# Regrouping float32r and float16 passes inside the gate products of a gated graph network on Trainium2

## The chip, the cores and the metric

The kernel runs on one core of one Trainium2 chip. The metric is the device time of one launch in microseconds (us); smaller is better. TensorE (PE in the profile) does the matrix products, ScalarE (ACT) and VectorE (DVE) the elementwise work, GpSimd (POOL) a little of it, and SyncE (SP) issues the transfers. PEld is the part of TensorE that loads a stationary operand (the weights of a matmul) into the array.

## What is computed

There are 64 graphs of 256 nodes with 256 features. A layer of three gated graph steps is followed by a graph attention layer; both begin with a layer norm and a ReLU and end with a residual. The gates of the gated steps are where the change lies:

```python
for i in range(3):
    m = einsum('bnd,de->bne', h, weight[i])
    aggr = einsum('bst,bsd->btd', A, m)          # A = (adj != 0)
    gi = aggr @ w_ih.T + b_ih ;  gh = h @ w_hh.T + b_hh
    r = sigmoid(i_r + h_r) ;  z = sigmoid(i_z + h_z)
    n = tanh(i_n + r * h_n)
    h = (1 - z) * n + z * h
...
e = leaky(h' @ a_left + (h' @ a_right).T), masked by adj
out = x + softmax(e) @ (h' @ W.T)
```

## The kernel before, in words

**Tiling.** The 64 graphs go in 32 pairs. For one pair, the state h is held transposed: two tiles (one for each block of 128 features, `db`) of 128 partitions by 512 columns, where the 512 columns are the 2 x 256 nodes of the two graphs. `weight[i] @ w_ih.T` is multiplied together once at the start, so that a gated step needs only the propagation by the adjacency matrix (`prop`, L807) and the gates. The stationary operand of a gate product is a 128 x 128 block of a weight matrix, and the moving operand is a 128 x 512 tile of the state. In the last gated step of the last pair the two graphs are done apart, so that the products there have 256 columns.

**Products in three parts.** A value v is split (`split16`, L655) into v0, which is rounded to float32r by ScalarE, a remainder v1 in float16 by VectorE (L660, L662), and a combination vd of both in float32r (L664). The weights are split likewise into `fac[m][:, 0]` (float32r), `low[m]` (float16) and `fac[m][:, 1]` (float32r). A gate (`gate`, L676) is then made of three operations on one PSUM bank:

- `top` (L683 to L686): for each term (the state's part `hh`, the aggregated part `i`, or both) and each of the two blocks `kb` of the contraction, a float32r matmul (j = 0) and a float16 matmul (j = 1), all accumulated in the bank. A top of one term has two of each kind; a top of two terms (gate z) has four of each.
- `scale` (L700): one ScalarE activation, in place, over the bank.
- `rest` (L688 to L691): two float32r matmuls for each term, accumulated on what `scale` left.

One `db` of one gated step has the gates r, nh, ni and z, where the top of r is made in two pieces (`topT`, `topF`): five tops, four scales and four rests. With 2 blocks, 3 steps and 32 pairs, and the last step of the last pair doubled, that is 970 tops, with 2,328 float32r and 2,328 float16 matmuls on L686, 582 scales in all and 2,328 float32r matmuls on L691. Gates r and z end in a Tanh on ScalarE (L826, L839); nh and ni go to VectorE (L831, L834), then to a Tanh (L836) and three VectorE operations (L843 to L847), which make the new state.

In the built program a float16 matmul stands as two instructions, a `Ldweights` and a `Matmult`; a float32r matmul is one instruction that loads its own weights. The profile shows a weight load (PEld) for both.

**What sets the order.** All operations are given to a planner (`Plan`) with an engine, an assumed duration, the buffers that they read and write, and a priority made of due times and a table of leads. `Plan.run` (L286) places them one by one, by the earliest start that its own durations give, and calls each operation's function at that moment; each engine executes its instructions in the order in which they were placed. So the order across gates is fixed when the program is built, and the tops, scales and rests of several gates, the propagation and the attention of other pairs lie interleaved on TensorE. The function `pe` (L431) registers a TensorE operation. The eight PSUM banks are one class of buffers of the planner (`bank`).

Of the kernel before, what the change touches and what calls it, by code (L numbers as in the profile page):

```python
# [353 lines left out]
def tile_gated_gnn_then_gat(  # L354
# [44 lines left out]
    DB = D // P  # L399
# [11 lines left out]
    plan = Plan(WINDOW, LEAD)  # L411
# [16 lines left out]

    def pe(name, n, fn, **kw):  # L431
        return plan.op(name, "PE", n, n + 220, fn, **kw)

    def act(name, n, fn, **kw):
        plan.op(name, "ACT", n, n + 170, fn, **kw)
# [54 lines left out]
    def setup():  # L490
# [6 lines left out]
        def load_rows():  # L497
# [4 lines left out]
        plan.op("rows", "ACT", 200, 3000, load_rows, w=[(rw, ONE)])  # L502
        pt = Buf("bank")
        pe("vec t", TR, lambda: nc.tensor.transpose(pt.t[:, :nrow], rw.t, ident[:nrow, :nrow]),
           r=[(rw, ONE), ("ident", ONE)], w=[(pt, ONE)])
        dve("vec", 70, lambda: nc.vector.tensor_copy(vec, pt.t[:, :nrow]), r=[(pt, ONE)], w=[("vec", ONE)])
# [14 lines left out]
        def transposed(dst, region, blocks, whole=None, up=1.0):  # L521

            def go_for(c):
                pt = Buf("bank")

                def go():
                    for r, (b, k) in enumerate(blocks):
                        nc.tensor.transpose(pt.t[:, ts(r, P)], parts(b)[:, k, ts(c, P)], ident)

                n = len(blocks)  # L530
                pe("w turn", TR * n, go, r=[(b, ONE) for b, _ in blocks] + [("ident", ONE)], w=[(pt, ONE)])
                w = n * P if whole is None else whole

                def copies():
                    nc.scalar.activation(dst(c)[:, :w], pt.t[:, :w], AF.Copy, scale=up)
                    if w < n * P:
                        nc.scalar.activation(dst(c)[:, w:], pt.t[:, w : n * P], AF.Copy, scale=0.5 * up)

                act("w copy", (140 if w == n * P else 260) + n * 110, copies, r=[(pt, ONE)], w=[region(c)])

            for c in range(DB):
                go_for(c)
# [46 lines left out]
        def bank_of(blocks, c):  # L589

            pt = Buf("bank")

            def go():
                for r, (b, k) in enumerate(blocks):
                    nc.tensor.transpose(pt.t[:, ts(r, P)], parts(b)[:, k, ts(c, P)], ident)

            pe("w turn", TR * len(blocks), go, r=[(b, ONE) for b, _ in blocks] + [("ident", ONE)], w=[(pt, ONE)])
            return pt
# [70 lines left out]
    def fit(ns, part):  # L669

        return ns if len(part) == 2 else 80 + 0.5 * ns

    def columns(part):
        return slice(part[0] * N, (part[-1] + 1) * N)

    def gate(name, e, terms, tops, apart=False, bias=0.0, part=ALL):  # L676

        bank = Buf("bank")
        half = e // 3
        cols, cost, cost16 = columns(part), PASS if len(part) == 2 else PROP, PASS16 if len(part) == 2 else PROP16  # L680
        f = lambda m, j, kb: low[m][:, kb, ts(e, P)] if j == 1 else fac[m][:, j // 2, kb, ts(e, P)]

        def top(terms, first):  # L683
            seq = [(m, j, kb, s[kb][j]) for m, s in terms for kb in range(DB) for j in range(2)]
            for n, (m, j, kb, b) in enumerate(seq):
                nc.tensor.matmul(bank.t[:, cols], f(m, j, kb), b.t[:, cols], start=(first and n == 0), stop=True, skip_group_check=True)  # L686

        def rest():  # L688
            for m, s in terms:
                for kb in range(DB):  # L690
                    nc.tensor.matmul(bank.t[:, cols], f(m, 2, kb), s[kb][2].t[:, cols], start=False, stop=True, skip_group_check=True)  # L691

        def reads(js, half_, terms=terms):
            return [(s[kb][j], ONE) for _, s in terms for kb in range(DB) for j in js] + [
                (f"fac{m}", tuple((kb, half, half_) for kb in range(DB))) for m, _ in terms]

        for ts_ in [terms[:1], terms[1:]] if apart and len(terms) > 1 else [terms]:
            tops.append(pe(name + " top" + (str(len(ts_) < len(terms) and ts_[0] is terms[0])[0]), 2 * (cost + cost16) * len(ts_), lambda ts_=ts_: top(ts_, ts_[0] is terms[0]),
                           r=reads((0, 1), 0, ts_), w=[(bank, ONE)]))
        act(name + " scale", fit(575 if "nh" in name else 515, part), lambda: nc.scalar.activation(  # L700
            bank.t[:, cols], bank.t[:, cols], AF.Identity, bias=bias, scale=SPLIT + 1.0), r=[("vec", ONE)], w=[(bank, ONE)])
        pe(name + " rest", 2 * cost * len(terms), rest, r=reads((2,), 1), w=[(bank, ONE)])
        return bank
# [361 lines left out]
```

## Time and profile before

The median of three runs is 2061.08 us (2057.64 to 2062.22). In the profiled execution the span is 2060.2 us, and the granted TensorE clock is 0.998 on average.

| What | Instructions | Busy us | Share of the span |
|---|---|---|---|
| TensorE, matmuls | 9,965 | 2039.5 | 99% |
| TensorE, weight loads | 9,965 | 1317.1 | 64% |
| ScalarE | 3,043 | 1744.2 | 85% |
| VectorE | 3,890 | 1699.6 | 82% |
| GpSimd | 198 | 147.8 | 7% |

A row of the profile's groups is read as: line, engine, operation, output<-inputs by the program's names without buffer numbers, shapes, count | busy us in all, mean ns of one | idle time of the engine just before, and what ended it. A row of the timeline has start (us from the beginning of the span), duration, and then the same names; neighbours of one kind are merged, with their number behind the x. float32r operands are shown as f32, with the tile name `round`. The recorded end of a matmul is modelled by the profiler, and matmuls are pipelined: the recorded duration of one is longer than the distance to the next. The pace of TensorE is therefore read from distances between neighbours, not from durations.

### The profile page before, as it was taken

What the parts mean: (1) busy time and instruction counts of PE and PEld (TensorE: products, weight loads), DVE (VectorE), ACT (ScalarE), POOL (GpSimd) and SP (SyncE); (2) the same over time, 40 slices, a digit from 0 to 9 for tenths busy, and PEclk for the clock granted to TensorE, in tenths of its full rate; (3) what the DMA queues carried; (4) which work ended last, traced back from release to release, by engine and by line L of the source; (5) the groups of instructions that cost most, each with busy time, mean ns of one, the idle gap of its engine ahead of it and who ended that gap; (6) DMA issues with size and microseconds to landing.
All of it is one profiled execution on the core that took longest, in us unless ns stands there. A gap on an engine that the chain in (4) does not pass through costs nothing. (4 is left out here: it accounts for less than half of the span.)

```text
span 2060.2 us, 31404 instructions
## 1 busy us (share of the span) xinstructions
PE 2039.5 (99%) x9965; PEld 1317.1 (64%) x9965; DVE 1699.6 (82%) x3890; ACT 1744.2 (85%) x3043; POOL 147.8 (7%) x198
## 2 busy tenths in 40 slices
PE   8999999999999999999999999999999999999998
PEld 5666666666666666666666656666666666666666
DVE  7678888888788888888888888888888888888886
ACT  6688888888888888888888888888888888888875
POOL 1000000000000000000000000000000000000000
PEclk9999999999999999999999999999999999999999
DMA  4137776677865677765677765678756778666632
GB/s 127 32 78 130 137 118 115 117 121 131 144 109 113 117 129 128 131 118 112 116 133 134 122 115 112 120 131 143 112 113 119 123 129 141 108 116 112 112 70 62
DMA packets 734472, 239.44 MB, mean 116 GB/s; under 512 B 658257, under 2 KB 734305, under 8 KB 734305
## 3 DMA queue, kind: packets, MB, share of 16 engines
q1 hardware_dynamic: 734272, 237.41, 65.3%
q8 instruction: 79, 1.29, 0.3%
q14 instruction: 89, 0.72, 0.1%
q10 hardware_dynamic: 32, 0.01, 0.0%
HBM read 61.09 MB, written 16.84 MB: 38 GB/s over the span
## 5 line engine op out<-in xcount | busy, mean ns | idle before, releaser
L686 PE MATMUL bank<-round,fac 128*128 128x512 f32 (+1 forms) x1164 | 551.1, 543 | 0.0
L686 PE MATMUL bank<-round,fac_hh 128*128 128x512 f32 (+1 forms) x1164 | 534.2, 522 | 0.0
L686 PE MATMUL bank<-half,low_hh 128*128 128x512 f16 (+1 forms) x1164 | 451.6, 388 | 0.0
L686 PE MATMUL bank<-half,low 128*128 128x512 f16 (+1 forms) x1164 | 450.5, 388 | 0.0
L691 PE MATMUL bank<-round,fac_hh 128*128 128x512 f32 (+1 forms) x1164 | 435.4, 455 | 0.6 <-ACT bank L700 0.4
L700 ACT ACTIVATE bank<-bank 128x512 f32<-128x512 f32 (+1 forms) x582 | 334.8, 580 | 116.3 <-PE bank L686 115.6
L691 PE MATMUL bank<-round,fac 128*128 128x512 f32 (+1 forms) x1164 | 367.3, 409 | 2.5 <-ACT bank L700 2.5
L724 ACT COPY full<-full 128x1024 uint16<-128x1024 uint16 x304 | 354.3, 1165 | 17.2 <-DMA full<-full 15.8
L686 PEld LDWEIGHTS <-low 128*128 128x128 f16 x1164 | 111.5, 96 | 293.8 <-issue 292.9
L686 PEld LDWEIGHTS <-low_hh 128*128 128x128 f16 x1164 | 111.8, 96 | 293.1 <-issue 291.6
L664 DVE SCALAR_TENSOR_TENSOR round<-half,round 128x512 fp32r<-128x512 f16 x384 | 260.4, 686 | 1.3
L691 PEld LDWEIGHTS bank<-round,fac 128*128 128x128 f32 x1164 | 216.5, 189 | 52.8 <-ACT bank L700 8.3
L686 PEld LDWEIGHTS bank<-round,fac_hh 128*128 128x128 f32 x1164 | 230.1, 198 | 14.6
L686 PEld LDWEIGHTS bank<-round,fac 128*128 128x128 f32 x1164 | 231.0, 198 | 8.7
L691 PEld LDWEIGHTS bank<-round,fac_hh 128*128 128x128 f32 x1164 | 211.5, 193 | 26.3 <-ACT bank L700 12.7
L746 POOL TENSOR_TENSOR small<-small,nhalf 128x2 f32<-128x2 f32 x128 | 114.4, 895 | 1526.3 <-DVE small L744 1456.0
L807 PE MATMUL bank<-round,round 128*128 128x256 f32 x1536 | 218.4, 291 | 0.3 <-DVE round L885 0.3
L831 DVE SCALAR_TENSOR_TENSOR full<-full,bank 128x512 f32<-128x512 f32 (+1 forms) x194 | 130.5, 673 | 106.9 <-ACT full L826 78.8
L845 DVE SCALAR_TENSOR_TENSOR full<-full,full 128x512 f32<-128x512 f32 (+1 forms) x194 | 132.3, 682 | 92.4 <-ACT full L839 92.0
L807 PEld LDWEIGHTS bank<-round,round 128*128 128x128 f32 x1536 | 201.2, 191 | 5.5 <-DVE round L885 0.5
L836 ACT ACTIVATE full<-full,vec 128x512 f32<-128x512 f32 (+1 forms) x194 | 136.3, 717 | 29.8 <-DVE full L834 29.7
L658 ACT ACTIVATE round<-bank 128x512 fp32r<-128x512 f32 x192 | 114.8, 598 | 49.6 <-PE bank L807 48.7
(108 smaller groups left out, 2958.8 us busy)
## 6 DMA issues: line engine op xcount, KB each, us to landing
full<-full SPq DMA_DIRECT2D x484, 128.0 KB, 3.5
x<-in_x_dram SPq DMA_DIRECT2D x64, 256.0 KB, 3.2
adj<-in_adj_dram SPq DMA_DIRECT2D x64, 256.0 KB, 5.2
full<-in_x_dram SPq DMA_DIRECT2D x64, 256.0 KB, 3.3
full<-full SPq DMA_DIRECT2D x248, 64.0 KB, 2.9
out_dram<-full SPq DMA_DIRECT2D x62, 256.0 KB, 2.5
full<-line SPq DMA_DIRECT2D x62, 128.0 KB, 3.8
full<-full SPq DMA_TRANSPOSE x304, 3.3
```

The source lines that it names most:

```text
L658: act(name + " 0", A512 if bank else C512, lambda: nc.scalar.activation(v0.t, v.t, AF.Copy, scale=up), r=[(v, ALL)], w=[(v0, ONE)])
L664: dve2(name + " d", V512, lambda: nc.vector.scalar_tensor_tensor(vd.t, v1.t, -SPLIT, v0.t.bitcast(F32), op0=ALU.mult, op1=ALU.add), r=[(v0 ...
L686: nc.tensor.matmul(bank.t[:, cols], f(m, j, kb), b.t[:, cols], start=(first and n == 0), stop=True, skip_group_check=True)
L691: nc.tensor.matmul(bank.t[:, cols], f(m, 2, kb), s[kb][2].t[:, cols], start=False, stop=True, skip_group_check=True)
L700: act(name + " scale", fit(575 if "nh" in name else 515, part), lambda: nc.scalar.activation(bank.t[:, cols], bank.t[:, cols], AF.Identity ...
L724: act(name, 1065, lambda: nc.scalar.copy(dst.t.bitcast(U16).rearrange("p (j n b) -> p j n b", j=2, b=2), src.t.bitcast(U16).rearrange(f"p ...
L746: pool(name + " pow", 900, lambda: nc.gpsimd.tensor_tensor(sm.t[:, 16:18], sm.t[:, 16:18], nhalf, ALU.pow), r=[("nhalf", ONE)], w=[(sm, (2 ...
L807: nc.tensor.matmul(pa.t[:, ts(g, N)], b, parts(A[g])[:, sb, :], start=(n == 0), stop=(n == len(terms) - 1))
L831: dve(f"u {db}{of}", fit(S512, part), lambda u=u, k=ph, b=r_, cols=cols: nc.vector.scalar_tensor_tensor(u.t[:, cols], b.t[:, cols], 1.0, k ...
L836: act(f"tanh {db}{of}", fit(615, part), lambda u=u, en=en, cols=cols: nc.scalar.activation(u.t[:, cols], u.t[:, cols], AF.Tanh, bias=b_i[: ...
L845: dve2(f"d mul {db}{of}", fit(V512, part), lambda d=d, b=z_, cols=cols: nc.vector.scalar_tensor_tensor(d.t[:, cols], b.t[:, cols], 1.0, d. ...
```

## The change

Before, the matmuls of a top alternate: for each term and each `kb`, a float32r matmul and then a float16 matmul. After, all matmuls of one kind in a top come first, then all of the other kind. A flag `narrow` remembers whether the last TensorE operation placed was a top that ended in float16; if so, the next top begins with its float16 matmuls, so that the two tops share one float16 group. Any TensorE operation that is not a top clears the flag. The purpose is to have TensorE change less often between the two kinds of operand. The assumed durations given to the planner are the same as before, and so are the number and the size of all instructions.

```diff
+    narrow = [False]
+
-    def pe(name, n, fn, **kw):
-        return plan.op(name, "PE", n, n + 220, fn, **kw)
+    def pe(name, n, fn, mixed=False, **kw):
+        def go():
+            fn()
+            narrow[0] = narrow[0] and mixed
+
+        return plan.op(name, "PE", n, n + 220, go, **kw)
...
         def top(terms, first):
-            seq = [(m, j, kb, s[kb][j]) for m, s in terms for kb in range(DB) for j in range(2)]
+            js = (1, 0) if narrow[0] else (0, 1)
+            narrow[0] = js[-1] == 1
+            seq = [(m, j, kb, s[kb][j]) for j in js for m, s in terms for kb in range(DB)]
             for n, (m, j, kb, b) in enumerate(seq):
                 nc.tensor.matmul(bank.t[:, cols], f(m, j, kb), b.t[:, cols], start=(first and n == 0), stop=True, skip_group_check=True)
...
-            tops.append(pe(name + " top" + ..., 2 * (cost + cost16) * len(ts_), lambda ts_=ts_: top(ts_, ts_[0] is terms[0]),
+            tops.append(pe(name + " top" + ..., 2 * (cost + cost16) * len(ts_), lambda ts_=ts_: top(ts_, ts_[0] is terms[0]), mixed=True,
                            r=reads((0, 1), 0, ts_), w=[(bank, ONE)]))
```

More of the change, by code (lines that the diff above doesn't have):

```diff
@@ L697, in gate @@
         for ts_ in [terms[:1], terms[1:]] if apart and len(terms) > 1 else [terms]:
-            tops.append(pe(name + " top" + (str(len(ts_) < len(terms) and ts_[0] is terms[0])[0]), 2 * (cost + cost16) * len(ts_), lambda ts_=ts_: top(ts_, ts_[0] is terms[0]),
+            tops.append(pe(name + " top" + (str(len(ts_) < len(terms) and ts_[0] is terms[0])[0]), 2 * (cost + cost16) * len(ts_), lambda ts_=ts_: top(ts_, ts_[0] is terms[0]), mixed=True,
                            r=reads((0, 1), 0, ts_), w=[(bank, ONE)]))
```

## The prediction

> **What bounds the kernel now.** I read the page's engine shares first, then who waits for whom, then the pace of TensorE in the timeline. The shares (engine, busy us, share, instructions):
>
> ```profile
> PE 2039.5 (99%) x9965; PEld 1317.1 (64%) x9965; DVE 1699.6 (82%) x3890; ACT 1744.2 (85%) x3043; POOL 147.8 (7%) x198
> ```
>
> 99% alone proves little, since pipelined matmuls overlap in the record. The waits decide (waiter <- releaser: us in all, times, longest):
>
> ```profile
> PEld L686 <- issue: 584.5, 2278, 0.4
> ...
> ACT bank L700 <- PE bank L686: 146.8, 262, 2.2
> ...
> PEld bank L691 <- ACT bank L700: 21.0, 86, 1.0
> ...
> PE bank L691 <- ACT bank L700: 2.9, 8, 0.5
> ```
>
> ScalarE waits 146.8 us for the tops; TensorE's matmul stream waits 2.9 us for the scales. The other engines follow TensorE. Differencing the recorded ends of all neighbouring matmuls gives the same: distances more than 20 ns over the median of their kind sum to 27 us, about 7.4 of them at 20 rests behind a scale, most others in the start and the last 50 us. So the time is a sum of matmul distances, and what counts is one distance. A steady stretch of TensorE:
>
> ```profile
> 1001.53 1.09 PE L691 MATMUL bank<-round,fac 128*128 128x512 f32 x4
> 1002.46 0.40 PE L686 MATMUL bank<-round,fac 128*128 128x512 f32 x1
> 1002.70 0.39 PE L686 MATMUL bank<-half,low 128*128 128x512 f16 x1
> 1002.74 0.58 PE L686 MATMUL bank<-round,fac 128*128 128x512 f32 x1
> 1003.17 0.39 PE L686 MATMUL bank<-half,low 128*128 128x512 f16 x1
> 1003.21 0.58 PE L686 MATMUL bank<-round,fac_hh 128*128 128x512 f32 x1
> ```
>
> Four float32r in a row take 1002.46 - 1001.53 = 0.93 us, 232.5 ns each. A float32r/float16 pair repeats after 1003.21 - 1002.74 = 0.47 (0.464 over five pairs), so a float16 matmul behind a float32r one also costs about 232. Over the whole trace, ends 2,280 times float32r to float16: mean 232.5, median 233 ns; float16 to float32r: 232.6, 233; float32r to float32r: median 234. Then the weight loads of the same stretch:
>
> ```profile
> 1002.70 0.10 PEld L686 LDWEIGHTS <-low 128*128 128x128 f16 x1 [0.28 <-issue]
> 1002.70 0.20 PEld L686 LDWEIGHTS bank<-round,fac 128*128 128x128 f32 x1
> 1003.16 0.10 PEld L686 LDWEIGHTS <-low 128*128 128x128 f16 x1 [0.26 <-issue]
> 1003.17 0.20 PEld L686 LDWEIGHTS bank<-round,fac_hh 128*128 128x128 f32 x1
> ```
>
> The float32r load starts together with the float16 matmul before its own (1003.17), a whole matmul early: hidden. The float16 load starts only 10 ns before its own matmul, after 0.26 us in which the loader did nothing; "issue" says that no semaphore held it. That is the row of 584.5 us in the waits, 2,278 of 2,328 float16 loads. Last, products of 256 columns, from the last pair:
>
> ```profile
> 2030.20 0.36 PE L686 MATMUL bank<-round,fac 128*128 128x256 f32 x1
> 2030.41 0.28 PE L686 MATMUL bank<-half,low 128*128 128x256 f16 x1
> 2030.45 0.36 PE L686 MATMUL bank<-round,fac_hh 128*128 128x256 f32 x1
> ```
>
> The pair takes 0.25 us here; over the trace float32r to float16 has a median of 126 ns, float16 to float32r 119. So float32r grows from 118 to 233 with its columns (0.45 ns a column, about 3 fixed), but float16 from 126 to 233, that is 0.418 ns a column and a fixed 19 ns.
>
> **What the skill says.** "TensorE: Matmul & The Clock Gate", section "Wait — 56ns, not 53.3ns?", puts warm matmuls of 512 columns 215.7 ns apart, start to start: 0.4167 ns a column and 2.5 fixed. My slope for float16 agrees, the fixed part does not: 19 against 2.5, so some 17 ns belong to something else. No float16 matmul stands behind another in this trace, so 215.7 is the page's, not measured here. The same page, "Step-by-step: what each phase is for", says that weight loads are pulled ahead of matmuls in flight, into a background buffer. The trace agrees for float32r, and disagrees for float16 behind float32r. The same page, "Weight-path perf modes", says that non-FP32 weights of 128 columns are loaded in a fast mode over four buses; the trace has 96 ns against about 190 to 200. "Perfetto Trace Analysis", section "Tensor Engine Instruction (MATMUL, LD_WEIGHTS)", says that matmul ends are estimated, which is why I trust distances.
>
> **The change, part by part.**
>
> Order. In the two built programs the instructions of ScalarE and VectorE stand in the same order with the same buffers; on TensorE only those inside tops move, and the number of instructions that carry a wait is the same for the tops (395) and the rests (826). Counting kinds in TensorE's order: before, 2,328 float16 groups of one matmul. After, 705 groups (345 of 2, 265 of 4, 91 of 6, 4 of 8), since 265 of the 970 tops begin with float16. That makes 2,328 - 705 = 1,623 places where float16 follows float16: 1,587 of 512 columns, 36 of 256.
>
> Price of a place. I take the 17 ns for the float16 load that cannot be pulled ahead of a float32r matmul; behind a float16 matmul it can (a float32r load does start early there). Then a float16 to float16 distance is 215.7 instead of 232.5: 16.8 saved. 1,587 x 16.8 = 26.7 us; 36 x (126 - 109) = 0.6 us. The 705 entries into a group stay at 233, and a float32r matmul costs the same behind either kind (233 or 234; 256 columns behind float16 117, behind float32r 118 to 119), so the new float32r neighbours cost nothing more. Sum: 27.3 us off TensorE. Bounds of the unknown distance: 213.3 (512 columns without any fixed part, by the page's slope) would give 1,587 x 19.2 + 0.6 = 31; 232.5 gives 0; a load that is fully exposed gives 215.7 + 96 = 312, 79 more for each place.
>
> Later or earlier operands. A regrouped top wants its second float32r operand one matmul earlier, a float16-first top wants its first float16 operand 0.23 us earlier, and at worst (gate z) its last one 4 x 0.23 = 0.93 us. Following each buffer in the trace, a float16 remainder is finished at least 0.5 us before its first use (median 5.5 us behind L660, 7.4 behind L662), and the float32r part at least 1.3 us. A wait there would hold the whole TensorE queue, but I count nothing: few are near the least.
>
> Given back at the scales. A rest needs its scale; behind the waiting rest stand all later tops, and ScalarE and VectorE wait for those. A quarter of the rests start within 0.31 us of the end of their scale, a tenth within 0.15, against a least of 0.05. TensorE becomes 27.3 / 2061 = 1.3% faster, ScalarE does not: its share rises from 85 to 86%. It has an idle moment at a top 262 times, about every 8 us, so between two of them TensorE runs ahead by at most 8 x 1.3% = 0.11 us. With some 60 rests (a tenth of 582) at the limit, that is 0 to 6.6 us; I take 3.
>
> Everything else (transfers, VectorE, GpSimd) is off the path, and hidden by TensorE, which waits for none of it in the steady part. Forecast: 2061.1 - 27.3 + 3 = 2036.8, say 2037 us.
>
> **The rivals.**
> 1. The 17 ns belong to the float16 matmul itself or to its separate load instruction, whatever stands before. For it: the load starts just in time in every pair, and the page's 215.7 does not say that weights are reloaded each time. Against it: the float32r load shows that the loader can work ahead under a float16 matmul. Then 0 saved: 2061, at most 2 us more by the earlier operands.
> 2. Full gain on TensorE, but the scales and the chain behind them (Tanh, VectorE, next state) take more than half of it. For it: the 86 delayed rest loads, 21.0 us. Against it: 146.8 us of ScalarE's own waiting. 2061 - 27 + 14 = 2048.
> 3. Slower: a separate float16 load behind a float16 matmul is not hidden at all. 1,623 x 79 = 128 us: 2189. Against it: the float32r loads again, and that the exposed part behind float32r is 17 of 96 ns. A milder form, no saving and new waits for the halves at the 265 float16-first tops, 30 ns each: 2069.
>
> **How the numbers follow.** Forecast (2031 to 2043) 0.63; rival 2 (2043 to 2056) 0.12; rival 1 (2057 to 2063) 0.13; rival 3 in both forms 0.12. The range goes from the lower bound, 2061 - 31 = 2030 and 1 us of waits, to 2062, which takes in rival 2 and nearly all of rival 1. Faster by over 0.2% (4 us): 0.75; within: 0.13; slower: 0.12.
>
> **What would show it.** In the changed trace a float16 row of x2 or x4 with 0.216 us between its matmuls, and float16 loads inside a group that start a matmul early, so that "issue" before them is left at about 705 places; pairs of graphs follow each other after about 61.5 instead of 62.3 us; rests wait for scales a little more than 2.9 us. The forecast is wrong if the distance inside a group stays at 232, or is near 310, or if waits at L691's successor grow past 10 us.

## The result, and the profile after

The changed kernel takes 2040.26 us (median of 4 runs, 2037.0 to 2042.54) against 2061.28 us before: ratio 0.990, 95% interval 0.9882 to 0.9919, 21 us less. The profiled span went from 2060.2 to 2039.3 us. One of the six runs of `short_after` (below) took 5210.29 us, for a reason that the record doesn't show, and is left out of its figures.

The page's shares, after:

```profile
span 2039.3 us, 31405 instructions
...
PE 2017.3 (99%) x9965; PEld 1434.3 (70%) x9965; DVE 1696.8 (83%) x3890; ACT 1741.0 (85%) x3043; POOL 147.7 (7%) x198
```

TensorE is as full as before; its work has become shorter by about what the span has. ScalarE and VectorE do the same work in the same time. The timeline of TensorE in a steady stretch, after (start, duration, what; x2 are two neighbours of one kind):

```profile
991.64 0.63 PE L694 MATMUL bank<-round,fac 128*128 128x512 f32 x2
992.11 0.60 PE L694 MATMUL bank<-half,low 128*128 128x512 f16 x2
992.55 0.59 PE L694 MATMUL bank<-half,low_hh 128*128 128x512 f16 x2
992.98 0.59 PE L694 MATMUL bank<-half,low 128*128 128x512 f16 x2
993.22 0.82 PE L694 MATMUL bank<-round,fac_hh 128*128 128x512 f32 x2
993.88 0.62 PE L694 MATMUL bank<-round,fac 128*128 128x512 f32 x2
```

Here is a shared group of six: from 992.55 to 992.98, two float16 matmuls take 0.43 us, 215 ns each. The weight loads of the same stretch:

```profile
992.10 0.12 PEld L694 LDWEIGHTS <-low 128*128 128x128 f16 x2 [0.28 <-issue]
992.33 0.31 PEld L694 LDWEIGHTS <-low_hh 128*128 128x128 f16 x2
992.76 0.31 PEld L694 LDWEIGHTS <-low 128*128 128x128 f16 x2
993.20 0.41 PEld L694 LDWEIGHTS bank<-round,fac_hh 128*128 128x128 f32 x2
```

Only the first load of the group has the 0.28 us of idle "issue" ahead of it and starts just in time (992.10 for a matmul at 992.11). Those for the matmuls at 992.55 and 992.98 start at 992.33 and 992.76, a matmul early. Over the trace, a float16 load starts 4 ns ahead of its matmul behind float32r, and 214 ns ahead behind float16. The waits of the whole trace (us, times, longest):

```profile
PEld L694 <- issue: 189.8, 693, 0.5
...
ACT bank L708 <- PE bank L694: 125.5, 232, 2.1
...
PEld bank L699 <- ACT bank L708: 31.7, 120, 1.3
...
PE bank L699 <- ACT bank L708: 3.3, 8, 0.9
```

The idle "issue" went from 2,278 to 693 places, one for each group but a few. The price is in the two last rows: loads of a rest that wait for a scale went from 86 to 120 times, 21.0 to 31.7 us.

The distances from the end of one matmul to the end of the next (512 columns, differences of recorded ends), summed over each trace:

| Neighbours | Before: count, mean ns, sum us | After |
|---|---|---|
| float32r, then float16 | 2,280, 232.5, 530.1 | 693, 231.7, 160.6 |
| float16, then float16 | none | 1,587, 215.8, 342.5 |
| float16, then float32r | 2,152, 232.6, 500.5 | 597, 237.5, 141.8 |
| float32r, then float32r | 2,182, 235.5, 513.9 | 3,737, 235.2, 878.9 |
| sum | 1,544.5 | 1,523.7 |

The sums differ by 20.8 us, which is nearly the whole change of the span (20.9); the distances next to products of other sizes sum to 507.8 us before and 507.6 after. Float16 matmuls, the first two rows, became 27.0 us cheaper; float32r matmuls, the last two, 6.3 us dearer.

### The profile page after: what moved, and what is told of

It reads as the page before. It is cut to its first block, busy times and chain, and to the rows that moved or that the text cites. A ratio compares the mean times of both kernels' runs of the same rounds, so it can differ in the third digit from the quotient of the medians.

```text
span 2039.3 us, 31405 instructions
## 1 busy us (share of the span) xinstructions
PE 2017.3 (99%) x9965; PEld 1434.3 (70%) x9965; DVE 1696.8 (83%) x3890; ACT 1741.0 (85%) x3043; POOL 147.7 (7%) x198
## 5 line engine op out<-in xcount | busy, mean ns | idle before, releaser
L699 PE MATMUL bank<-round,fac_hh 128*128 128x512 f32 (+1 forms) x1164 | 421.6, 443 | 1.1 <-ACT bank L708 0.6
L694 PE MATMUL bank<-round,fac_hh 128*128 128x512 f32 (+1 forms) x1164 | 399.1, 425 | 0.0
L694 PE MATMUL bank<-round,fac 128*128 128x512 f32 (+1 forms) x1164 | 376.3, 409 | 0.0
L732 ACT COPY full<-full 128x1024 uint16<-128x1024 uint16 x304 | 354.4, 1166 | 21.5 <-DMA full<-full 20.8
L699 PE MATMUL bank<-round,fac 128*128 128x512 f32 (+1 forms) x1164 | 358.1, 401 | 3.0 <-ACT bank L708 2.7
L694 PE MATMUL bank<-half,low_hh 128*128 128x512 f16 (+1 forms) x1164 | 343.1, 382 | 0.0
L694 PE MATMUL bank<-half,low 128*128 128x512 f16 (+1 forms) x1164 | 336.1, 380 | 0.0
L699 PEld LDWEIGHTS bank<-round,fac 128*128 128x128 f32 x1164 | 214.2, 188 | 65.0 <-ACT bank L708 15.0
L699 PEld LDWEIGHTS bank<-round,fac_hh 128*128 128x128 f32 x1164 | 207.2, 189 | 68.7 <-ACT bank L708 16.8
L694 PEld LDWEIGHTS bank<-round,fac 128*128 128x128 f32 x1164 | 216.0, 188 | 54.5
L694 PEld LDWEIGHTS bank<-round,fac_hh 128*128 128x128 f32 x1164 | 214.9, 190 | 52.7
L815 PE MATMUL bank<-round,round 128*128 128x256 f32 x1536 | 213.0, 288 | 0.3 <-DVE round L893 0.3
L694 PEld LDWEIGHTS <-low 128*128 128x128 f16 x1164 | 91.0, 98 | 144.8 <-issue 76.3
L694 PEld LDWEIGHTS <-low_hh 128*128 128x128 f16 x1164 | 80.5, 98 | 151.2 <-issue 113.5
```

Of the source, the lines that this page charges most:

```text
L732: act(name, 1065, lambda: nc.scalar.copy(dst.t.bitcast(U16).rearrange("p (j n b) -> p j n b", j=2, b=2), src.t.bitcast(U16).rearrange(f"p ...
L815: nc.tensor.matmul(pa.t[:, ts(g, N)], b, parts(A[g])[:, sb, :], start=(n == 0), stop=(n == len(terms) - 1))
```

## The experiments

**The theory:** each float16 matmul behind another saves some 17 ns of TensorE, because its weight load can then be pulled ahead; behind float32r it can't. **Rivals:** a fixed cost for changing the kind of operand; a gain from the sharing across tops; costs from operands wanted earlier. And where the full 27.3 us did not arrive: waits for scales, or dearer distances elsewhere.

### The change again, and the regrouping without sharing

`again` is the changed kernel, unedited, run once more beside the next three.

> The changed kernel once more, beside the others of this group. Both theories: 2040 us, ratio to before 0.990. It gives the size against which the next two are read.

It took 2041.03 us against 2060.58 before, ratio 0.9905 (0.9892 to 0.9919), 1 us more than expected.

`in_top` regroups in each top, but every top begins with float32r:

```diff
-            js = (1, 0) if narrow[0] else (0, 1)
-            narrow[0] = js[-1] == 1
+            js = (0, 1)
```

> Regrouped inside each top, but no group is shared between tops: 970 float16 groups in place of 705 (before: 2,328), so 1,358 places with float16 behind float16 in place of 1,623. If the gain is a fixed saving for each such place, in proportion to the 20.4 us measured for 1,623: 17 us saved, 2044 us, ratio 0.9917; distance float16 to float16 216 ns. Rival, the sharing across tops brings most (because it also moves operands and scales): 2050 or more. Rival, the sharing costs by wanting operands earlier: 2040 or less.

Measured: 2041.16 us, ratio 0.9905 (0.9892 to 0.9919), the same as with sharing. The distance float16 to float16 is 216 ns (median of 1,330). So 19 us come from the grouping inside tops, and the sharing added nothing that can be measured in the time, though it has 265 more cheap places, worth 4.4 us. The proportional saving forecast 2044 us, which lies 3 us above the measured time; its ratio, 0.9917, is still inside the interval, and the 2040 of the last rival is as near.

The traces show where the 4.4 us went. In the distances of 512 columns (the sum of the table above, waits at rests included) sharing keeps 1 to 2 us: 1525.7 in `in_top`, 1523.7 and 1524.5 in the two profiles with sharing. Waits take back the rest of it. Distances over 20 ns above the median of their kind sum to 26.6 us in `in_top` (27.1 before), and to 31.7 and 31.0 with sharing. Of these 4 to 5 us, 2.0 to 2.4 stand at rests; 1 to 3 lie in the first 40 and the last 50 us of the span, and whether sharing causes those isn't shown. The waits of `in_top`:

```profile
PEld L693 <- issue: 260.9, 950, 0.5
...
ACT bank L707 <- PE bank L693: 129.3, 238, 2.2
...
PEld bank L698 <- ACT bank L707: 29.3, 109, 1.1
```

950 places of "issue" stand between the 2,278 of before and the 693 of after, as the groups do, and so do the 109 delayed loads of rests between 86 and 120.

### float16 first, alternating

```diff
-            seq = [(m, j, kb, s[kb][j]) for m, s in terms for kb in range(DB) for j in range(2)]
+            seq = [(m, j, kb, s[kb][j]) for m, s in terms for kb in range(DB) for j in (1, 0)]
```

> Alternating as before, but float16 ahead of float32r in every pair. 2,328 float16 groups of one, so no float16 behind float16. If only these places save: 2061 us, ratio 1.000, within 0.2%. Rival, wanting the float16 remainder one matmul earlier makes waits that the changed kernel paid for: slower by 2 to 8 us.

Measured: 2059.32 us, ratio 0.9997 (0.9989 to 1.0005), as expected if only these places save. Wanting the remainder one matmul earlier costs nothing, and alternation in either order saves nothing. Its trace shows one thing more. Some tops here stand behind a plain float32 matmul (L958, tile name `full`), so that float16 follows a matmul that is neither float16 nor float32r. TensorE and then the loads:

```profile
1857.80 1.46 PE L958 MATMUL bank<-full,full 128*128 128x256 f32 x6
1859.10 0.38 PE L686 MATMUL bank<-half,low_hh 128*128 128x512 f16 x1
1859.13 0.58 PE L686 MATMUL bank<-round,fac_hh 128*128 128x512 f32 x1
1859.55 0.39 PE L686 MATMUL bank<-half,low_hh 128*128 128x512 f16 x1
```

```profile
1858.88 0.10 PEld L686 LDWEIGHTS <-low_hh 128*128 128x128 f16 x1
1859.10 0.19 PEld L686 LDWEIGHTS bank<-round,fac_hh 128*128 128x128 f32 x1
1859.54 0.10 PEld L686 LDWEIGHTS <-low_hh 128*128 128x128 f16 x1 [0.26 <-issue]
```

Behind plain float32 the float16 load starts 0.22 us early (1858.88 for 1859.10); behind float32r, a few lines on, 0.01 us early, with the idle "issue". The end-to-end distances follow: 215 or 216 ns in all 29 places behind 256-column float32, 233 (median) behind float32r. So it is not any change of kind that costs 17 ns, and it is the places with a late load that pay.

### Scales made short

ScalarE's scale is done on 128 of 512 columns, so that TensorE waits for it less; the rest of the bank stays unscaled. ScalarE as a whole has less to do too: its share of the span falls from 85 to 75%.

```diff
-            bank.t[:, cols], bank.t[:, cols], AF.Identity, bias=bias, scale=SPLIT + 1.0), ...
+            bank.t[:, cols][:, :128], bank.t[:, cols][:, :128], AF.Identity, bias=bias, scale=SPLIT + 1.0), ...
```

This edit was made to the kernel before (`short_before`), to the changed kernel (`short_after`, and again as `short_after2`) and to the regrouping without sharing (`short_in_top`).

> The kernel before, with the scale after each top done on 128 of its 512 columns only (the other columns are left unscaled), so that a scale takes about 0.23 us in place of 0.58. The distances inside the tops are untouched. About 7 us of rests waiting for scales go: 2054 us, ratio 0.9965.

> The changed kernel with the same short scale. If what was missing from 27.3 us was given back at rests that wait for scales: the difference to the kernel before with the short scale grows from 20.9 us (between the two profiled spans) to 25 to 27, 2028 us. Rival, it is lost at dearer distances between float32r neighbours or elsewhere: the difference stays at 20 to 23, 2032 us.

> Regrouped inside each top, no sharing, with the scale on 128 of 512 columns (the others unscaled). Sharing across tops brought nothing measurable with the full scale (2041.16 against 2041.03). If its 257 places were given back at waits for scales, it shows here: 4 us slower than the changed kernel with the short scale, about 2033.5. Rival, shared groups don't save TensorE time at all: the same time as the changed kernel with the short scale, 2029.5.

> The changed kernel with the short scale again, beside the one above on the same chip: 2029.5 us in both theories.

| Kernel | us | Ratio to the kernel before | 95% interval |
|---|---|---|---|
| short_before | 2055.08 | 0.9979 | 0.9969 to 0.9988 |
| short_after | 2028.56 | 0.9847 | 0.9834 to 0.9860 |
| short_in_top | 2034.19 | 0.9879 | 0.9864 to 0.9893 |
| short_after2 | 2030.97 | 0.9861 | 0.9845 to 0.9877 |

The page's row of the scale, and the waits for it, in `short_after`:

```profile
L708 ACT ACTIVATE bank<-bank 128x128 f32<-128x128 f32 x582 | 150.0, 262 | 172.2 <-PE bank L694 171.0
```

```profile
PEld bank L699 <- ACT bank L708: 7.4, 14, 1.3
```

A scale of this row takes 262 ns in place of 581, and delayed rest loads are down from 120 to 14. `short_before` gained 4.6 us (2059.67 to 2055.08), less than the 7 expected.

With short scales the change is worth 2055.08 - 2028.56 = 26.5 us; with `short_after2`, by its ratio, (0.9979 - 0.9861) x 2060 = 24.3 us. With full scales it was 19.6 to 21.0. The expectation of 25 to 27 was met by the first run and just missed by the second, so waits for scales did take a part of the missing us. The traces show a smaller part than the times do:

| Sums over the trace, us | Full scale: before, after, again | Short scale: before, after, after2 |
|---|---|---|
| Distances of 512 columns (as in the table above) | 1544.5, 1523.7, 1524.5 | 1540.4, 1517.3, 1518.0 |
| Distances next to other sizes | 507.8, 507.6, 507.1 | 505.2, 501.5, 503.7 |
| At rests, over 20 ns above the median | 8.9, 12.7, 13.1 | 3.3, 5.4, 5.2 |

The change adds 3.8 to 4.2 us of waits at rests with full scales and 1.9 to 2.1 with short ones, and in the distances of 512 columns it is worth 20.0 to 20.8 us with full scales and 22.4 to 23.1 with short ones. So about 2 us are shown to come back when the scale is short. The rest of the difference lies in the second row, which moves by up to 4 us between kernels with the same scale, and these runs don't tell why.

Sharing, too, shows here: 2034.19 against 2030.97, 3.2 us, near the 4 expected if its gain is eaten by waits for scales, and far from none. In the distances of 512 columns it is 2.6 to 3.3 us (1520.6 in `short_in_top`). But the intervals of the two ratios overlap a little, so its size is not settled.

### What the 17 ns are: weights of 64 columns

`m64_alt` gives the float16 matmuls of the kernel before weights of 64 columns, the others keep 128; `m64_grp` does so in `in_top`:

```diff
-                nc.tensor.matmul(bank.t[:, cols], f(m, j, kb), b.t[:, cols], ...)
+                o = 64 if j == 1 else P
+                nc.tensor.matmul(bank.t[:o, cols], f(m, j, kb)[:, :o], b.t[:, cols], ...)
```

> The kernel before, alternating, with float16 weights of 64 columns in place of 128 (the float16 products fill only half of the output rows; the other half lacks them). If the extra 17 ns behind a float32r matmul are the exposed part of the weight load, the distance float32r to float16 changes with the size of the load: 225 or less if the load is cut in half, 240 or more if loads below 128 columns are slower. Rival, a fixed cost of changing the kind of operand: the distance stays at 232 to 233.

> Regrouped inside each top, no sharing, with float16 weights of 64 columns (again only half of the output rows get the float16 products). If the load behind a float16 matmul is hidden: float16 to float16 stays at 216 whatever its length, and float32r to float16 is as in the alternating kernel with 64 columns. Rival, part of the load shows there too: float16 to float16 moves as well.

They took 2750.68 and 2321.29 us (one run each). float32r to float16 went from 233 to 333 ns, float16 to float32r to 433 (`m64_alt`) and 430 (`m64_grp`), float16 to float16 stayed at 216. The distance behind float32r did leave 233, against the rival. But here the shape changes between neighbours as well, and that alone could keep loads back. So in `all64_alt` and `all64_grp` all matmuls of tops and rests have 64 weight columns (the banks are cleared once at the start):

```diff
+                nc.tensor.matmul(bank.t[:64, cols], f(m, j, kb)[:, :64], b.t[:, cols], ...)
...
+                    nc.tensor.matmul(bank.t[:64, cols], f(m, 2, kb)[:, :64], s[kb][2].t[:, cols], ...)
```

> The kernel before, alternating, with 64 weight columns in all matmuls of the tops and rests (half of the gates' output rows are left out), so that [...]the shape doesn't change between neighbours. If the 17 ns are a float16 load that shows: float32r to float16 leaves 233 (up to 333 if all of a 64-column load shows, as it did in the kernel that mixes 64 and 128 columns). Rival, a fixed cost for leaving float32r: it stays at 233. Float32r to float32r 233 in both.

> Regrouped inside each top, 64 weight columns in all matmuls of tops and rests (half of the gates' output rows are left out). Float16 to float16 216 with loads that start about 214 ns ahead in both theories; float32r to float16 as in the alternating kernel of 64 columns.

They took 2625.81 and 2267.27 us (one run each). The timeline of TensorE in `all64_alt`, then its loads:

```profile
1001.08 0.45 PE L686 MATMUL bank<-round,fac_hh 128*64 128x512 f32 x1
1001.46 0.40 PE L686 MATMUL bank<-half,low_hh 128*64 128x512 f16 x1
1001.80 0.45 PE L686 MATMUL bank<-round,fac_hh 128*64 128x512 f32 x1
1002.18 0.40 PE L686 MATMUL bank<-half,low_hh 128*64 128x512 f16 x1
```

```profile
1001.08 0.13 PEld L686 LDWEIGHTS bank<-round,fac_hh 128*64 128x64 f32 x1 [0.23 <-issue]
1001.46 0.11 PEld L686 LDWEIGHTS <-low_hh 128*64 128x64 f16 x1 [0.25 <-issue]
1001.79 0.13 PEld L686 LDWEIGHTS bank<-round,fac_hh 128*64 128x64 f32 x1 [0.23 <-issue]
```

float32r to float16 is 333 ns without any change of shape (median of 2,280), float32r to float32r 230, float16 to float16 216 in `all64_grp` (1,330 places, loads 214 ns ahead). The moving operands of 512 columns are the same as before, and only the number of weight columns was altered; the cost behind float32r went from 17 to 117 ns, and the recorded load there takes 106 (median). A cost for leaving float32r that is the same whatever the weights is ruled out: with 64 columns, what shows is about one load. That the 17 ns of this kernel are likewise the part of a late load that shows is the natural reading, but it is argued from the late start and from `h_first`, not shown by itself. Why a load of 128 float16 columns, recorded with 96 ns, shows so little of itself, these runs don't tell.

### Longer runs of tops

The planner takes a top that is ready at most 300 ns later instead of another TensorE operation when an unshared float16 group has just ended (`NEAR`, 40000, bounds by how much it may go against the priorities):

```diff
             (t, _, _), o = best
+            if o.eng == "PE" and self.narrow[0] and " top" not in o.name:
+                ...                 # tq: earliest start of each waiting top
+                if near is not None and near[0][0] - o.prio < NEAR:
+                    o = near[1]
```

> The change, and in addition the planner takes a ready top (or one ready within 300 ns of its reckoning) before another TensorE operation when an unshared float16 group has just ended. 640 groups in place of 705: 65 x 17 ns = 1.1 us less of TensorE, 2039 us, if only the groups count. Rival, the table of leads belongs to the order that it was made for and the scales come later for the rests: slower than the changed kernel, 2045 to 2070.

Measured: 2138.15 us, ratio 1.0389 (1.0371 to 1.0407). It has 640 groups, so 1.1 us less to do by their count; it takes 97 us more than `again`, and lies beyond the 2045 to 2070 of the rival. The shares and two rows of its waits:

```profile
PE 2053.0 (96%) x9965; PEld 1444.3 (68%) x9965; DVE 1722.9 (81%) x3890; ACT 1745.8 (82%) x3043; POOL 143.3 (7%) x198
```

```profile
PE bank L713 <- ACT round L683: 14.9, 22, 1.1
PE bank L718 <- ACT bank L727: 14.4, 29, 2.1
```

TensorE is 96% busy and now waits for ScalarE's part of the split (L683) and for scales (L727), among others. Distances over 20 ns above the median of their kind sum to 128.7 us in place of 31.0 in `again`: the whole loss is waits, and float16 to float16 is 216 ns (median) here too. That the table of leads belongs to the old order is the likely reason for the waits, but only argued. Of the kernels that compute the whole result none beats the changed one; `in_top` equals it with less code.

## Why the prediction was right

**What bounds the kernel.** Right. The matmul distances of 512 columns account for 20.8 of 20.9 us.

**The price of a place.** Right: 215.8 ns measured for 215.7 taken from the Trainium skill, "TensorE: Matmul & The Clock Gate", section "Wait — 56ns, not 53.3ns?", so 16.7 ns for each of 1,587 places, 26.5 us, and 109 against 126 (medians) for the 36 of 256 columns. The reason given fits all that was measured: the float16 load behind float32r is not pulled ahead, and that behind float16 or plain float32 is; that the 17 ns are the part of the late load that shows stays argued. The same page, section "Step-by-step: what each phase is for", makes this pulling ahead depend on the row groups and on the background buffer, and does not name the exception that float32r makes here.

**New float32r neighbours cost nothing more.** A little wrong. I compared medians over all places. Between matmuls of tops alone, with places over 20 ns above the median left out, float32r behind float16 was 230.8 ns before (1,687 places), and float32r behind float32r is 232.5 after (1,430): 1.7 x 1,430 = 2.4 us. Where a shared group ends and the next float32r begins, it is 234.1 (257 places): 3.3 x 257 = 0.8 us more. Other float32r places, such as the first matmul of a rest, became about 1 us cheaper in all, so 2.2 us are left.

**Earlier operands.** Right: no float16-first top waits for its remainder in the steady part, and alternation with float16 first costs nothing.

**Given back at the scales.** Right in kind. Places over 20 ns at rests went from 8.9 to 12.7 us (13.1 in `again`), 3.8 to 4.2 us for the 3 taken. But the 3 was picked between bounds and not worked out, so that it came this near is luck. One bound was also wrong. It used a tenth of 582 scales, and 582 leaves out the scales of gate nh, which the profile lists by themselves (kernel before, `--source L700`):

```profile
L700 ACT ACTIVATE bank<-bank,b_nh x194: 445/662/707, 28.7 to 2019.2; 128x512 f32<-128x512 f32 x190, 128x256 f32<-128x256 f32 x4
```

There are 776 scales in all, so a tenth is 78 and the upper bound 8.6 us in place of 6.6. Nothing else in the argument rests on the 582.

**The sum.** In the distances of 512 columns: 27.0 us saved at float16 matmuls (26.7 forecast), 4.1 given back in places over 20 ns at float32r matmuls, nearly all of them rests (3 forecast), 2.2 at the other float32r matmuls (none forecast), which leaves 20.7. The table has 20.8, and the times 19.6 to 21.0; 24.3 was forecast. The terms that were mis-sized are the float32r neighbours and the waits, both taken too small. The time of 2040.26 us lies in the first band, 2031 to 2043, but the whole range goes to 2062 and takes in rival 2 and most of rival 1, so that lying in it proves little. The 216 ns, the early loads and the 693 places of "issue" decide between the theories.

**The rivals.** Rival 1 and both forms of rival 3 fell with the 216 ns. Rival 2 named a real loss, but about 4 of the 27 us and not more than half.

**What I did not ask.** Whether the 265 shared tops were worth having: by count they were 4.4 of 27.3 us, in the time none that shows, and about 3 us where scales are short.

## What to carry to other kernels

Where TensorE is the bound and its matmuls change between float32r and float16, put those of one kind in a row inside an accumulation: it costs no instruction, and here it took 1% off, about 17 ns for each float16 matmul that no longer stands behind float32r. Other two-byte types were not run. Read the gain from the distance between ends of neighbouring matmuls and from where each weight load starts, not from busy shares. A part of the gain (here about 4 of 27 us) can be lost where another engine stands just behind TensorE, so look for the waits that are near their limit before going further.

## What the runs showed that was not expected

- Not every load is pulled ahead: with 128 float16 columns a load starts 214 ns before its matmul behind float16 and behind plain float32, and 4 ns before it behind float32r.
- With 64 weight columns it is worse: between float32r and float16 no load is pulled ahead in either direction, so that float32r to float16 takes 333 ns and float16 to float32r 380, though such loads are recorded with 106 and 133 ns. The alternating kernel with half of the gate products' output rows took 2625.81 us, 28% more than the whole one.
- Mixing 64 and 128 columns makes float16 to float32r dearer still: 433 ns.
